# Cross-attention block on one Trainium2 core: pairs of maxima and sums in one tile, combined by VectorE instructions with one operand, in a new order of the steps

## The chip, the core and the metric

The kernel runs on one core of one Trainium2 chip. The core has five engines that each take their instructions in the order of the program: TensorE (PE; its weight loads are shown as PEld), VectorE (DVE), ScalarE (ACT), GpSimd (POOL) and SyncE (SP), which issues nearly all DMA transfers. They wait for one another through semaphores. The metric is the device time of one execution in microseconds (us), as a median over runs.

## The reference

Inputs: `x` (16 samples x 1024 rows x 512), a context of 64 rows for each sample, a condition vector for each sample, and weights. Everything is fp32.

```python
xq  = ada_ln(x,   cond, Wss_q,  bss_q)     # (1 + scale) * layernorm(x) + bias,
xkv = ada_ln(ctx, cond, Wss_kv, bss_kv)    # [scale, bias] = silu(cond) @ Wss + bss
q = (xq @ Wq + bq)                          # 16 heads of 32
k, v = split(xkv @ Wkv + bkv)
attn = softmax(q @ k.T / sqrt(32))          # over the 64 context rows
out  = x + ((attn @ v) @ Wp + bp)
```

## The kernel before

**Tiling.** `x` is cut into 32 blocks of 512 rows (`NB = 32`; block i is half of sample i // 2). The context is handled in two groups, A and B, of eight samples. A block's features are turned so that features lie on the partitions: normalised by `hidden` (L351), transposed in squares of 32 by `turn` (VectorE, L373), moved to their partitions by 16 small transfers in `move` (L392), and scaled and shifted by `scale_features` (ScalarE, L453).

**Products.** Each 512 x 512 product (query, key, value and the projection at the end) is computed as seven half-size products instead of eight, so there is a `query_product(i, n)` and a `product(i, n)` with n = 1 to 7. The price is sums and differences of quarters: `feature_sums` and `row_sums` on GpSimd, sums of weights once. Results gather in two PSUM banks for each kind: query products 1, 6, 5, 3 add into one bank, 2 and then 7, 4 into the other, and between them `query_out` (ScalarE, L583) reads a partial result or `query_added` (VectorE, L592) adds one. A product that adds into a bank waits for the reader before it. `query_seed` copies product 1 into the second bank. In the projection, `biased` and `product_seed` set the banks, `take` (ScalarE) copies partial results out, `joined` (GpSimd) or `added` (VectorE) adds them to the residual rows, and with n = 3 or 4 the finished rows are sent out.

**Softmax.** The scores of a block come in two halves w (`score_products(i, w)`, L662), each with two tiles e of two PSUM banks. The 64 context rows of a head lie on 64 partitions, two groups of 32. `maximum(i, z, e)` (L685) transposes 32x32 squares and takes the maximum over each group of 32, so there are two maxima for each query, one for each group. `copied` (L694) copies the scores out of PSUM. `exchanged(i, w)` (L722) lets ScalarE copy each group's maxima to the partitions of the other group, in four copies. `maxima(i, w)` (L732) combines the two by one VectorE instruction (L735) and spreads the result to all rows (L715). Then `subtract` (GpSimd, L739) and `weights` (exponential on ScalarE, L743). `row_total` (L749) sums over each group of 32, `sums_moved` (L762) brings the two groups' sums side by side through a round trip to DRAM, and `inverse` (L776) adds them by one instruction (L779) and takes the reciprocal (L780). `spread_rows` spreads it, `mix` (L810) multiplies weights and values on TensorE, and `divided` scales the result into `ot`, the input of the projection.

**The order.** No scheduler runs: the list of calls at the end of the function is the order of the program, and so of each engine. It has a way in (from L980: context A, keys and values, blocks 0 to 2 in part), a loop over i = 3 to 29 (L1440) and a way out (L1550, blocks y = 30 and z = 31). In a loop pass, block i has its softmax, block n = i + 1 its query product, block a = i - 1 its `mix` and most of its projection, b = i - 2 its last two projection products (3 and 4), f = i + 2 its scaling and feature differences, and blocks i + 3 to i + 5 their loading, statistics and turning. `product` 3 and 4 of block b are the second and the fourth product of a pass.

Tile buffers are few: two each for rows of `x` and for residual rows, one for the turned block `ht`, two for `xt`. The two tiles of a half's scores and the two results of `mix` share the same four PSUM banks, so `mix` waits until both score tiles were copied and their maxima taken.

## Time and profile before

| what | value |
|---|---|
| median of 3 runs | 1033.63 us (1032.38 to 1034.6) |
| the profiled execution | 1034.3 us; its span in the trace 1032.5 us |
| busy: TensorE, VectorE, GpSimd, ScalarE | 994.3, 941.0, 811.0, 779.1 us |
| mean granted TensorE clock | 0.995 |
| transfers | 151.7 MB, mean 147 GB/s |

How to read it: the profile is one execution. A row of the timeline gives the start (us from the span's start), the length, the engine, the line of the kernel, the operation, output<-inputs by tile name, and in square brackets how long the engine had been idle and what ended that. A row of the groups gives the shapes, the number of instructions, the busy time in us with the mean of one in ns, and the idle time just before them. A row of the stretches gives for each stretch the length, then the busy time of PE, PEld, DVE, ACT and POOL, the granted clock, the share of the DMA engines and GB/s. A matmul's end is modelled, and each of the program's matmuls in fp32 shows as two instructions: a half-size product is 8.

### The profile page before, as it was taken

What the parts mean: (1) busy time and instruction counts of PE and PEld (TensorE: products, weight loads), DVE (VectorE), ACT (ScalarE), POOL (GpSimd) and SP (SyncE); (2) the same over time, 40 slices, a digit from 0 to 9 for tenths busy, and PEclk for the clock granted to TensorE, in tenths of its full rate; (3) what the DMA queues carried; (4) which work ended last, traced back from release to release, by engine and by line L of the source; (5) the groups of instructions that cost most, each with busy time, mean ns of one, the idle gap of its engine ahead of it and who ended that gap; (6) DMA issues with size and microseconds to landing.
All of it is one profiled execution on the core that took longest, in us unless ns stands there. A gap on an engine that the chain in (4) does not pass through costs nothing.

```text
span 1032.5 us, 17757 instructions
## 1 busy us (share of the span) xinstructions
PE 994.3 (96%) x6060; PEld 759.1 (74%) x6060; DVE 941.0 (91%) x1170; ACT 779.1 (75%) x1426; POOL 811.0 (79%) x603
## 2 busy tenths in 40 slices
PE   6997999999999999999999999999999999999988
PEld 5875867777777777777777777777777778777657
DVE  4687999899999999999999999999999999987995
ACT  3687746788888888888878788888878788876641
POOL 1565676888888889888888889888888888887773
PEclk9999999999999999999999999999999999999989
DMA  9484633644555444544555544445554454334123
GB/s 315 146 211 114 175 102 119 186 140 139 165 168 143 134 146 154 162 130 148 166 169 129 147 148 149 157 121 164 166 165 134 127 160 157 122 113 126 44 90 125
DMA packets 111802, 151.70 MB, mean 147 GB/s; under 512 B 29624, under 2 KB 45008, under 8 KB 111712
## 3 DMA queue, kind: packets, MB, share of 16 engines
q1 hardware_dynamic: 111024, 149.75, 47.8%
q8 instruction: 48, 0.79, 0.3%
q0 software_dynamic: 256, 0.52, 0.2%
q14 instruction: 42, 0.34, 0.1%
q10 hardware_dynamic: 432, 0.30, 0.1%
HBM read 80.26 MB, written 35.65 MB: 112 GB/s over the span
## 4 chain that ended last, share of the span: by engine, by line
PE 57%; DVE 20%; issue 9%; ACT 8%; DMA 5%; SPq 1%; POOL 0%; DVEq 0%; ACTq 0%
PE pp L918 27%; PE pq L551 22%; DVE m L686 12%; ACT qt L590 4%; PE ps L669 3%; ACT mo L728 2%; DVE m L735 2%; DVE iv L780 1%; DMA x<-in_x_dram 1%; PE pv_B L551 1%; DVE lt L752 1%; PE pk_A L551 1%; DVE iv L779 1%; PE po L820 1%; DMA V_A<-stage_A 1%
## 5 line engine op out<-in xcount | busy, mean ns | idle before, releaser
L739 POOL TENSOR_TENSOR s<-s,mb 128x2048 f32<-128x2048 f32 x64 | 290.7, 4542 | 65.0 <-DVE iv L779 41.7
L695 ACT COPY s<-ps 128x1024 f32<-128x1024 f32 x128 | 129.2, 1011 | 97.2 <-DVE m L686 69.6
L918 PE MATMUL pp<-w_p_sb,ot 128*128 128x256 f32 x760 | 181.1, 382 | 6.6 <-DVE ot L806 6.6
L918 PEld LDWEIGHTS pp<-w_p_sb,ot 128*128 128x128 f32 x760 | 145.0, 191 | 29.1 <-DVE ot L806 5.4
L686 DVE TRANSPOSE_TENSOR_REDUCE m<-ps 128x32 f32<-128x1024 f32 x128 | 152.3, 1221 | 6.0 <-PE ps L669 3.1
L964 POOL TENSOR_TENSOR r<-r,taken 128x512 f32<-128x512 f32 x116 | 147.0, 1278 | 13.7 <-ACT taken L959 11.5
L715 DVE STREAM_TRANSPOSE mb<-m 128x2048 f32<-128x2048 f32 x64 | 147.9, 2312 | 7.0 <-DVE m L735 0.5
L752 DVE TRANSPOSE_TENSOR_REDUCE lt<-s 128x64 f32<-128x2048 f32 x64 | 143.5, 2273 | 1.1 <-ACT s L743 1.1
L551 PE MATMUL pq<-xt,w_q_sums 128*128 128x256 f32 x512 | 124.5, 386 | 8.1 <-ACT qt L590 8.0
L551 PEld LDWEIGHTS pq<-xt,w_q_sums 128*128 128x128 f32 x512 | 95.3, 191 | 46.3 <-ACT qt L590 32.7
L743 ACT ACTIVATE s<-s 128x2048 f32<-128x2048 f32 x64 | 122.0, 1909 | 6.0 <-POOL s L739 5.3
L551 PE MATMUL pq<-xt,w_q_sb 128*128 128x256 f32 x512 | 124.3, 386 | 1.5 <-ACT pq L563 1.5
L918 PE MATMUL pp<-WT,ot 128*128 128x256 f32 x512 | 123.8, 385 | 0.0
L551 PEld LDWEIGHTS pq<-xt,w_q_sb 128*128 128x128 f32 x512 | 94.6, 190 | 39.2 <-ACT pq L563 24.4
L551 PE MATMUL pq<-xt_sums,w_q_sums 128*128 128x256 f32 x512 | 120.8, 379 | 1.7 <-POOL xt_sums L507 1.1
L918 PE MATMUL pp<-WT,s 128*128 128x256 f32 x512 | 121.2, 379 | 0.0
L918 PEld LDWEIGHTS pp<-WT,ot 128*128 128x128 f32 x512 | 94.6, 189 | 35.0 <-issue 21.3
L590 ACT ACTIVATE qt<-pq,bias_t 128x256 f32<-128x256 f32 x256 | 104.0, 476 | 7.0 <-PE pq L551 6.9
L551 PEld LDWEIGHTS pq<-xt_sums,w_q_sums 128*128 128x128 f32 x512 | 97.1, 190 | 15.6 <-POOL xt_sums L507 1.5
L918 PEld LDWEIGHTS pp<-WT,s 128*128 128x128 f32 x512 | 97.1, 190 | 14.3 <-DVE m L735 0.8
L456 ACT ACTIVATE xt<-xt,ss_q 128x512 f32<-128x512 f32 x124 | 97.4, 809 | 6.3 <-DMA xt<-ht 6.3
L347 ACT ACTIVATE x<-x,rstdq 128x512 f32<-128x512 f32 x128 | 100.2, 808 | 2.0 <-POOL rstdq L322 1.7
(172 smaller groups left out, 1601.9 us busy)
## 6 DMA issues: line engine op xcount, KB each, us to landing
x<-in_x_dram SPq DMA_DIRECT2D x32, 1024.0 KB, 6.3
r<-in_x_dram SPq DMA_DIRECT2D x32, 1024.0 KB, 5.1
out_dram<-r SPq DMA_DIRECT2D x62, 512.0 KB, 3.7
xt<-ht SPq DMA_DIRECT2D x488, 64.0 KB, 2.4
wss_kv<-in_L_xcond_Wss_kv_dram SPq DMA_DIRECT2D x4, 512.0 KB, 8.0
wss_q<-in_L_xcond_Wss_q_dram SPq DMA_DIRECT2D x4, 512.0 KB, 8.2
ltd<-lt SPq DMA_DIRECT2D x32, 64.0 KB, 1.5
vr<-ltd SPq DMA_DIRECT2D x126, 16.0 KB, 1.7
```

The costliest lines, as they stand in the source:

```text
L347: nc.scalar.activation(dst, src, AF.Identity, bias=rstd[:, 1, j : j + 1], scale=rstd[:, 0, j : j + 1])
L456: nc.scalar.activation(xt[:, :, c, :], xt[:, :, c, :], AF.Identity, scale=ss["q"][:, c, b : b + 1], bias=ss["q"][:, NC + c, b : b + 1],)
L551: nc.tensor.matmul(out_, lhsT=lhsT, rhs=rhs, start=new and m == 0 and c == 0, stop=c == HC - 1, skip_group_check=True,)
L590: nc.scalar.activation(dst, src, AF.Identity, bias=bq_t[:, o : o + 1])
L686: nc.vector.tensor_reduce(m_tiles[i][:, z, 2 * e : 2 * e + 2, :], s_banks[i, z][e].rearrange("p r (j a) -> p r j a", a=32), AX.X, ALU.max, ...
L695: nc.scalar.copy(s_tiles[i, z][:, 2 * e : 2 * e + 2, :], s_banks[i, z][e])
L715: nc.vector.transpose(t, src.unsqueeze(2).to_broadcast([P, HPC * NJ, 32]))
L739: eng.tensor_tensor(s_tiles[i, w], s_tiles[i, w], mb_tiles[i, w], ALU.subtract)
L743: nc.scalar.activation(p, p, AF.Exp, scale=SCALE)
L752: nc.vector.tensor_reduce(lt_tiles[i][:, :, w, :], s_tiles[i, w].rearrange("p r (j a) -> p r j a", a=32), AX.X, ALU.add, apply_transpose=True,
L918: nc.tensor.matmul(acc[products_of(i, n)][:, t * HO : (t + 1) * HO], lhsT=rows[:, c, t * P : (t + 1) * P], rhs=cols[:, c, :], start=new an ...
L964: nc.gpsimd.tensor_add(r, r, taken[i][:, slot, :].rearrange("p (t h) -> p t h", t=2))
```

## The change

The tile of maxima `m2` gets one more dimension: place 0 holds a partition's own maxima, place 1 the ones that `exchanged` copies from the other group (before: two tiles, `m2` and `mo`). `maxima` combines the two places by `both` (L704, which was there and unused): a `tensor_reduce` over the pair, with one operand, in place of a `tensor_tensor` with two. `inverse` adds its two halves in the same way. All steps are the same otherwise, but the way in, the loop and the way out are listed in a new order; the same calls are made, each once. The transfers are issued at new places too: in the loop `load_x`, `sums_moved`, `move` and `load_residual` follow each other in this order at the end of a pass (before: `load_residual`, `sums_moved`, `load_x`, `move`); in the way in, half of V's move to its place (`value_move("A", 0)`) comes behind `move(2)` instead of ahead of it.

In the diff, the way in is cut to its start and two places further on, and the way out to the part around `inverse(y)` and `mix(y)`.

```diff
@@ -674,7 +674,7 @@
                     stop=True,
                 )
         if i not in m_tiles:
-            m_tiles[i] = small.tile([P, 2, HPC, NJ], F32, tag="m2", name=f"m2_{i}", bufs=2)
+            m_tiles[i] = small.tile([P, 2, 2, HPC, NJ], F32, tag="m2", name=f"m2_{i}", bufs=2)
         if i < NB - 1:
             pool, tag = big, f"big{i % 2 * 2 + w}"
         else:
@@ -684,7 +684,7 @@
 
     def maximum(i, z, e):
         nc.vector.tensor_reduce(
-            m_tiles[i][:, z, 2 * e : 2 * e + 2, :],
+            m_tiles[i][:, z, 0, 2 * e : 2 * e + 2, :],
             s_banks[i, z][e].rearrange("p r (j a) -> p r j a", a=32),
             AX.X,
             ALU.max,
@@ -717,22 +717,15 @@
 
     mb_tiles = {}
 
-    mo_tiles, mb_tiles = {}, {}
-
-    def exchanged(i, w, e=None):
-        if i not in mo_tiles:
-            mo_tiles[i] = small.tile([P, 2, HPC, NJ], F32, tag="mo", name=f"mo_{i}", bufs=2)
-        rs = slice(0, HPC) if e is None else slice(2 * e, 2 * e + 2)
+    def exchanged(i, w):
+        t = m_tiles[i][:, w]
         for k in range(4):
             o = k ^ 1
-            nc.scalar.copy(
-                mo_tiles[i][32 * o : 32 * o + 32, w, rs], m_tiles[i][32 * k : 32 * k + 32, w, rs]
-            )
+            nc.scalar.copy(t[32 * o : 32 * o + 32, 1], t[32 * k : 32 * k + 32, 0])
 
     def maxima(i, w):
         m = small.tile([P, HPC * NJ], F32, tag="m", name=f"m_{i}_{w}", bufs=2)
-        a, b = (t[i][:, w].rearrange("p r j -> p (r j)") for t in (m_tiles, mo_tiles))
-        nc.vector.tensor_tensor(m, a, b, ALU.max)
+        both(m, m_tiles[i][:, w], ALU.max)
         mb_tiles[i, w] = spread(i, m, f"mb_{i}_{w}")
 
     def subtract(i, w, eng=nc.gpsimd):
@@ -776,7 +769,7 @@
     def inverse(i):
         v = halves.pop(i)
         t = small.tile([P, 2, 2 * NJ], F32, tag="iv", name=f"iv_{i}", bufs=2)
-        nc.vector.tensor_tensor(t, v[:, :, 0], v[:, :, 1], ALU.add)
+        nc.vector.tensor_reduce(t, v.rearrange("p d z j -> p d j z"), AX.X, ALU.add)
         nc.vector.reciprocal(t, t)
         vt_rows[i] = t.rearrange("p d (w j) -> p d w j", w=2)
@@ -977,465 +970,465 @@
+    condition_turned()
+    load_first(2, 2)
     q_stats("A", (0,))
+    q_stats("A", (1,))
+    warm_up(12)
+    warm_up(6)
+    first_scale(0)
+    load_scale_shift("kv", w_ss_kv, 0, (0,))
+    load_context_weights(0, 0, 0)
+    q_stats("A", (2,))
+    hidden("A", (1,))
+    q_stats("A", (3,))
+    silu()
+    first_scale(1)
+    hidden("A", (0,))
+    turned_features("A", 0)
+    hidden("A", (2,))
+    load_scale_shift("kv", w_ss_kv, 0, (1,))
+    scale_shift_rows("kv", 0)
+    hidden("A", (3,))
+    scale_shift_taken("kv", 0)
+    load_context_weights(0, 0, 1)
+    turned_features("A", 3)
+    load_context_weights(1, 0, 0)
+    load_scale_shift("kv", w_ss_kv, 1, (0,))
     load_biases(0)
-    load_scale_shift("kv", w_ss_kv, 0, (0,))
-    condition_turned()
-    silu()
-    q_stats("A", (1,))
-    first_scale(0)
-    load_first(2, 2)
-    hidden("A", (1,))
-    hidden("A", (0,))
-    q_stats("A", (3,))
-    load_scale_shift("kv", w_ss_kv, 0, (1,))
-    q_stats("A", (2,))
-    turned_features("A", 0)
-    load_context_weights(1, 0, 0)
-    first_scale(1)
+    biases(0)
+    load_scale_shift("kv", w_ss_kv, 1, (1,))
     turned_features("A", 1)
-    scale_shift_rows("kv", 0)
-    load_scale_shift("kv", w_ss_kv, 1, (0,))
-    scale_shift_taken("kv", 0)
-    hidden("A", (2,))
-    load_context_weights(0, 0, 0)
-    warm_up(12)
-    load_scale_shift("kv", w_ss_kv, 1, (1,))
-    warm_up(6)
-    biases(0)
     scale_shift("kv", 2 * NC, 0)
-    modulated("A", 0, 0, nc.scalar)
-    turned_features("A", 2)
-    hidden("A", (3,))
     scale_shift_rows("kv", 1)
+    load_x(0)
     modulated("A", 0, 0, nc.vector)
     scale_shift_taken("kv", 1)
+    scale_shift("kv", 2 * NC, 1)
+    modulated("A", 0, 0, nc.scalar)
+    modulated("A", 1, 0, nc.vector)
+    turned_features("A", 2)
+    load_context_weights(1, 0, 1)
+    modulated("A", 0, 1, nc.scalar)
...
+    turn(2, (0,))
+    context_out("B", "k", 1)
+    hidden(2, (2,))
+    value_move("A", 1)
+    load_projection_bias()
+    score_products(0, 0)
+    scale_features(1, (0,))
+    scale_features(1, (1,))
+    scale_features(1, (3,))
+    scale_features(1, (2,))
+    turn(2, (2,))
+    feature_sums(1, nc.gpsimd, (0,))
+    feature_sums(1, nc.gpsimd, (1,))
+    maximum(0, 0, 0)
+    load_x(4)
+    context_product("B", "k", 2)
+    copied(0, 0, 0)
+    maximum(0, 0, 1)
+    context_product("B", "k", 6)
+    q_stats(3, (0,))
+    q_stats(3, (2,))
+    move(2)
+    q_stats(3, (1,))
+    query_product(1, 1)
+    copied(0, 0, 1)
+    exchanged(0, 0)
...
+    turn(3, (2,))
+    turn(3, (0,))
+    context_product("B", "k", 3)
+    query_out(1, 7)
+    query_added(1, 5)
+    scale_features(2, (3,))
     hidden(3, (3,))
-    query_product(1, 7)
-    move(2)
-    copied(0, 1, 1)
-    q_stats(4, (0,))
-    q_stats(4, (3,))
-    query_out(1, 6)
-    hidden(3, (0,))
-    maxima(0, 1)
-    scale_features(2, (3,))
-    q_stats(4, (1,))
-    query_product(1, 5)
-    query_out(1, 7)
-    turn(3, (2,))
+    context_product("B", "k", 4)
+    scale_features(2, (1,))
...
@@ -1443,254 +1436,254 @@
 
         score_products(i, 0)
         product(b, 3)
+        maximum(i, 0, 0)
+        query_product(n, 1)
         copied(i, 0, 1)
-        query_product(n, 1)
-        maximum(i, 0, 0)
+        added(b, 3)
         maximum(i, 0, 1)
+        if next_x:
+            q_stats(i + 4, (1,))
+        product(b, 4)
         copied(i, 0, 0)
         exchanged(i, 0)
-        added(b, 3)
+        score_products(i, 1)
+        query_seed(n)
         maxima(i, 0)
-        product(b, 4)
-        biased(a, 2)
-        if more:
-            hidden(i + 3, (3,))
-        score_products(i, 1)
+        maximum(i, 1, 0)
         inverse(a)
-        maximum(i, 1, 0)
         if more:
             hidden(i + 3, (1,))
         maximum(i, 1, 1)
-        query_seed(n)
-        copied(i, 1, 0)
+        subtract(i, 0)
         query_product(n, 2)
         query_product(n, 6)
-        copied(i, 1, 1)
-        subtract(i, 0)
+        query_out(n, 2)
+        query_product(n, 7)
+        copied(i, 1, 0)
+        if more:
+            hidden(i + 3, (3,))
         spread_rows(a)
         added(b, 4)
+        copied(i, 1, 1)
         mix(a)
         divided(a, (0,))
         row_sums(a, 0, (0,))
         divided(a, (1,))
+        exchanged(i, 1)
+        query_out(n, 7)
+        query_out(n, 6)
+        maxima(i, 1)
+        biased(a, 2)
+        weights(i, 0)
         row_sums(a, 1, (0,))
-        query_out(n, 2)
-        query_out(n, 6)
-        query_product(n, 5)
-        product(a, 1)
-        exchanged(i, 1)
-        weights(i, 0)
-        product_seed(a)
-        maxima(i, 1)
         if more:
             hidden(i + 3, (0,))
-        scale_features(f, (1,))
-        scale_features(f, (2,))
-        query_product(n, 7)
+        query_product(n, 4)
+        product(a, 1)
+        product_seed(a)
+        query_product(n, 5)
+        if more:
+            hidden(i + 3, (2,))
+        scale_features(f, (0,))
         if next_x:
             q_stats(i + 4, (0,))
         if more:
-            hidden(i + 3, (2,))
-        row_sums(a, 0, (1,))
-        subtract(i, 1)
+            turn(i + 3, (2,))
+        product(a, 2)
+        scale_features(f, (2,))
+        take(a, 2, 0)
+        if i == NB - 3:
+            load_residual(NB - 1)
         if more:
             turn(i + 3, (0,))
+        product(a, 6)
+        row_sums(a, 0, (1,))
+        query_added(n, 5)
+        biased(a, 3)
+        take(a, 6, 2)
+        query_product(n, 3)
+        if more:
+            turn(i + 3, (3,))
+        product(a, 5)
+        subtract(i, 1)
+        scale_features(f, (1,))
+        joined(a, 2, 0)
+        joined(a, 6, 2)
+        row_sums(a, 1, (1,))
         if next_x:
-            q_stats(i + 4, (1,))
+            q_stats(i + 4, (2,))
         if more:
             turn(i + 3, (1,))
-        if next_x:
-            q_stats(i + 4, (2,))
-        product(a, 6)
-        take(a, 6, 2)
-        query_out(n, 7)
-        product(a, 2)
-        take(a, 2, 0)
-        joined(a, 2, 0)
-        query_added(n, 5)
-        biased(a, 3)
-        joined(a, 6, 2)
-        load_residual(i)
-        product(a, 5)
+        product(a, 7)
         weights(i, 1)
         take(a, 5, 3)
-        scale_features(f, (3,))
-        if more:
-            turn(i + 3, (2,))
-        row_total(i, 0)
-        product(a, 7)
-        row_total(i, 1)
-        query_product(n, 3)
-        joined(a, 5, 3)
-        take(a, 7, 1)
-        sums_moved(i)
-        joined(a, 7, 1)
-        scale_features(f, (0,))
-        query_out(n, 3)
-        feature_sums(f, nc.gpsimd, (0,))
-        row_sums(a, 1, (1,))
         if next_x:
             q_stats(i + 4, (3,))
-        query_product(n, 4)
-        if more:
-            turn(i + 3, (3,))
+        query_out(n, 3)
         if i < NB - 5:
             load_x(i + 5)
-        if i == NB - 3:
-            load_residual(NB - 1)
+        joined(a, 5, 3)
+        scale_features(f, (3,))
+        row_total(i, 0)
+        take(a, 7, 1)
+        joined(a, 7, 1)
+        if next_x:
+            q_scale(i + 4)
+        row_total(i, 1)
+        feature_sums(f, nc.gpsimd, (0,))
         feature_sums(f, nc.gpsimd, (1,))
         query_added(n, 4)
-        if next_x:
-            q_scale(i + 4)
+        feature_sums(f, nc.gpsimd, (2,))
+        feature_sums(f, nc.gpsimd, (3,))
+        sums_moved(i)
         if i + 3 < NB:
             move(i + 3)
-        feature_sums(f, nc.gpsimd, (2,))
-        feature_sums(f, nc.gpsimd, (3,))
+        load_residual(i)
 
...
+    row_sums(y - 1, 0, (1,))
+    copied(z, 0, 0)
+    take(y - 1, 1, 0)
+    exchanged(z, 0)
+    product(y - 1, 2)
     subtract(y, 0)
-    copied(z, 0, 0)
-    product(y - 2, 4)
+    weights(y, 0)
+    take(y - 1, 2, 1)
+    row_total(y, 1)
+    maxima(z, 0)
     score_products(z, 1)
-    row_sums(y - 1, 0, (1,))
     row_sums(y - 1, 1, (0,))
-    exchanged(z, 0)
-    row_total(y, 1)
-    weights(y, 0)
-    maxima(z, 0)
-    product(y - 1, 2)
+    joined(y - 1, 1, 0)
     row_total(y, 0)
-    subtract(z, 0)
-    take(y - 1, 1, 0)
-    take(y - 1, 2, 1)
     product(y - 1, 6)
-    product(y - 2, 3)
-    biased(y - 1, 3)
     sums_moved(y)
-    take(y - 1, 6, 3)
     maximum(z, 1, 1)
     maximum(z, 1, 0)
+    product(y - 2, 4)
+    added(y - 2, 4)
+    take(y - 1, 6, 3)
+    subtract(z, 0)
+    load_residual(y)
+    biased(y - 1, 3)
     copied(z, 1, 1)
     exchanged(z, 1)
-    added(y - 2, 4)
-    added(y - 2, 3)
+    product(y - 1, 7)
+    row_sums(y - 1, 1, (1,))
+    maxima(z, 1)
+    joined(y - 1, 2, 1)
+    copied(z, 1, 0)
+    weights(z, 0)
+    inverse(y)
+    spread_rows(y, (0,))
+    take(y - 1, 7, 2)
+    spread_rows(y, (1,))
+    mix(y)
     biased(y, 2)
-    product(y - 1, 7)
-    maxima(z, 1)
     product(y - 1, 5)
-    inverse(y)
-    copied(z, 1, 0)
-    joined(y - 1, 1, 0)
-    spread_rows(y, (0,))
-    joined(y - 1, 2, 1)
-    row_sums(y - 1, 1, (1,))
-    mix(y)
+    product(y - 1, 4)
+    divided(y, (0,))
     take(y - 1, 5, 1)
-    spread_rows(y, (1,))
+    divided(y, (1,))
     subtract(z, 1)
     product(y - 1, 3)
-    divided(y, (0,))
+    product(y, 1)
     row_sums(y, 0, (0,))
-    divided(y, (1,))
-    weights(z, 0)
-    take(y - 1, 7, 2)
+    weights(z, 1)
+    row_total(z, 0)
+    product(y, 2)
+    row_sums(y, 1, (0,))
+    row_total(z, 1)
+    row_sums(y, 0, (1,))
     joined(y - 1, 7, 2)
-    row_sums(y, 1, (0,))
-    weights(z, 1)
-    product(y - 1, 4)
-    load_residual(y)
-    row_total(z, 0)
-    product(y, 1)
-    row_total(z, 1)
     added(y, 1)
+    row_sums(y, 1, (1,))
+    added(y, 2)
+    biased(y, 3)
+    joined(y - 1, 5, 1)
+    joined(y - 1, 6, 3)
```

715 lines of the change are left out of this document (341 added, 374 removed).

## The prediction

> **What bounds the kernel now.** I read the stages first: each engine's busy time in five stretches cut at starts of score products. The first ends where the first context product starts, the second is the rest of the way in, the third is loop pass i=3, the fourth passes 4 to 29, the last the way out.
>
> ```profile
> core 0: us, PE busy (x) PEld busy (x) DVE busy (x) ACT busy (x) POOL busy (x), PEclk, DMA share, GB/s
> 0.00:19.28 19.28, 9.56 (x101) 7.88 (x102) 9.03 (x33) 5.18 (x12) 1.14 (x7) 1.00 0.92 303
> 19.28:166.88 147.60, 139.35 (x808) 110.94 (x807) 124.88 (x206) 103.34 (x217) 95.95 (x90) 0.99 0.56 159
> 166.88:195.61 28.73, 28.73 (x177) 21.98 (x176) 25.71 (x32) 22.81 (x38) 20.41 (x15) 1.00 0.52 150
> 195.61:954.91 759.30, 749.54 (x4578) 569.84 (x4577) 719.79 (x842) 616.96 (x1109) 644.91 (x465) 1.00 0.48 147
> 954.91:1032.50 77.59, 67.13 (x401) 48.49 (x400) 61.61 (x59) 30.84 (x51) 48.60 (x29) 0.96 0.25 86
> ```
>
> TensorE is the bound everywhere. Pass 3 has no gap and takes 28.73 us; the 26 passes behind it take 759.30/26 = 29.20, with 759.30 - 749.54 = 9.76 us of gaps, 0.375 each. VectorE is next (719.79/26 = 27.7 a pass), then GpSimd (24.8) and ScalarE (23.7). So an order of the loop can gain about 10 us at most; the way in has 8.25 us of gaps behind its first product, the way out 10.46. Then who TensorE waited for between 200 and 920 us:
>
> ```profile
> PE pq L551 <- ACT qt L590: 7.6, 24, 0.4
> PE pq L551 <- ACT pq L563: 1.5, 1, 1.5
> ```
>
> The first row is one place in every pass. The timeline of a pass shows it, and then the same place in pass 3, where nothing waits:
>
> ```profile
> 463.21 1.27 POOL L507 TENSOR_TENSOR xt_sums<-xt 128x512 f32<-128x512 f32 x1
> 463.73 0.83 DVE L735 TENSOR_TENSOR m<-m,mo 128x64 f32<-128x64 f32 x1 [0.49 <-ACT mo L728]
> 466.53 1.99 PE L551 MATMUL pq<-xt,w_q_sb 128*128 128x256 f32 x8
> 468.81 2.14 ACT L695 COPY s<-ps 128x1024 f32<-128x1024 f32 x2 [2.48 <-DVE m L686]
> 470.18 1.95 PE L820 MATMUL po<-s,V_A 64*32 64x512 f32 x32
> 470.84 1.57 ACT L590 ACTIVATE qt<-pq,bias_t 128x256 f32<-128x256 f32 x4
> 472.47 1.99 PE L551 MATMUL pq<-xt,w_q_sums 128*128 128x256 f32 x8 [0.34 <-ACT qt L590]
> ...
> 178.00 1.95 PE L820 MATMUL po<-s,V_A 64*32 64x512 f32 x32
> 179.88 1.99 PE L551 MATMUL pq<-xt,w_q_sums 128*128 128x256 f32 x8
> ```
>
> Query product 5 behind `mix` adds into the bank that `query_out(n, 6)` reads. That read stands behind the two score copies, these behind the maxima, these behind the combination on L735, which took 0.83 us and ended at 464.56, just behind GpSimd's instruction (464.48). From `mix` to the product it is 2.29 us, without a wait 1.88.
>
> **The operation.** All executions of the two instructions that change (minimum, median, maximum in ns), then the nearest rows to what replaces them:
>
> ```profile
> L735 DVE TENSOR_TENSOR m<-m,mo x64: 193/398/1280, 82.8 to 987.7; 128x64 f32<-128x64 f32 x64
> L779 DVE TENSOR_TENSOR iv<-vr x32: 180/182/4576, 117.8 to 1012.2; 128x64 f32<-128x64 f32 x32
> L752 DVE TRANSPOSE_TENSOR_REDUCE lt<-s x64: 2267/2270/2311, 95.0 to 1002.7; 128x64 f32<-128x2048 f32 x64
> L735 DVE TENSOR_TENSOR m<-m,mo 128x64 f32<-128x64 f32 x64 | 36.2, 565 | 13.7 <-ACT mo L728 13.7
> L279 DVE COPY early<-ps_kv 128x128 f32<-128x128 f32 x2 | 0.6, 292 | 0.9 <-PE ps_kv L266 0.9
> L780 DVE RECIPROCAL iv<-iv 128x64 f32<-128x64 f32 x32 | 17.7, 553 | 1.1
> ```
>
> The form of two operands costs 0.19 us alone and up to 4.58 beside a GpSimd instruction. A reduction of one operand (L752) never strays by over 0.05 us, though GpSimd is busy for 85% of the loop. The trace has no reduction of pairs, 128x64<-128x128. Bounds: 0.19 (L735 alone) and 0.55 (L780, the slowest with 64 results); I take 0.29 from L279, which reads as many elements. VectorE saves 64 x (0.565 - 0.29) = 17.6 us, 0.55 a pass; the sums, mostly 0.18 now, lose 0.1 us each except the one of 4.58. VectorE isn't the bound, so this counts only through the chain above and the one of the way out. `exchanged` issues the same four 32x64 copies to another place: nothing changes on ScalarE.
>
> [...]
>
> **The loop, -6 us.** The new order puts query product 7 ahead of `mix` and product 4 behind it; 4 adds into the bank that `query_out(n, 7)` reads. Between the end of product 2 and that read, ScalarE does two output halves, a score copy, a normalisation, a score copy, four exchange copies and two output halves, by these means:
>
> ```profile
> L695 ACT COPY s<-ps 128x1024 f32<-128x1024 f32 x128 | 129.2, 1011 | 97.2 <-DVE m L686 69.6 <-PE ps L669 21.4
> L743 ACT ACTIVATE s<-s 128x2048 f32<-128x2048 f32 x64 | 122.0, 1909 | 6.0 <-POOL s L739 5.3
> L590 ACT ACTIVATE qt<-pq,bias_t 128x256 f32<-128x256 f32 x256 | 104.0, 476 | 7.0 <-PE pq L551 6.9
> L347 ACT ACTIVATE x<-x,rstdq 128x512 f32<-128x512 f32 x128 | 100.2, 808 | 2.0 <-POOL rstdq L322 1.7
> L728 ACT COPY mo<-m 32x64 f32<-32x64 f32 x256 | 61.9, 242 | 14.4 <-DVE m L686 11.0
> ```
>
> That is 0.95 + 1.01 + 0.81 + 1.01 + 0.97 + 0.95 = 5.70 us; four output halves back to back take 1.57 instead of 1.90 (470.84), so 5.0 is as likely. On the clock of the pass above: product 2 ends at 468.52, ScalarE is through between 473.5 and 474.2. TensorE is there at 466.53 + three products (1.73 each, 8 instructions of 216 ns) + 1.88 = 473.6. So product 4 waits 0 to 0.6 us; I take 0.15, against 0.375 now: 26 x 0.22 = 6. At the bounds the loop gains 9.8 or loses 6.
>
> What else moves in a pass, at nothing: (a) `added(b, 3)` stands between the first two maxima. Its product ends some 0.7 us behind the first maximum, so VectorE idles that long and the statistics and combination behind it are later; VectorE has 27.7 - 0.55 + 0.7 = 27.9 us to do in 28.9, and without that cover each 0.1 us is 2.6 us in all. (b) `query_out(n, 3)`, which the next score product needs, gets two products (3.45 us) for cover instead of one. (c) On SP, `sums_moved` and the 16 transfers of `move` now come ahead of `load_residual(i)`. That load of 1 MB is thus issued about 16 us into the next pass (16 such transfers took 13.51 us in a row below) and lands 5 us later; its first reader, `joined(a, 2, 0)`, stands behind `subtract(i, 1)` on GpSimd, about 23.7 us into the pass. If it came late, GpSimd and the row differences behind it would wait. (d) The feature differences go in a row at the end: GpSimd has about 3.9 us a pass to spare.
>
> **The way out, -3 us.** Timeline, and the granted clock (second figure from the end but one) behind the gap:
>
> ```profile
> 990.73 4.53 POOL L739 TENSOR_TENSOR s<-s,mb 128x2048 f32<-128x2048 f32 x1
> 990.76 4.58 DVE L779 TENSOR_TENSOR iv<-vr 128x64 f32<-128x64 f32 x1 [0.17 <-DMA vr<-ltd]
> 999.49 3.78 PE L918 MATMUL pp<-w_p_sb,ot 128*128 128x256 f32 x8 [5.04 <-DVE ot L806]
> ...
> 999.45:1006.00 6.55, 6.51 (x41) 3.18 (x41) 6.10 (x4) 0.58 (x1) 6.48 (x6) 0.57 0.02 6
> ```
>
> The sum of the halves of block 30 stood for a whole GpSimd subtraction, and inverse, spreading, division and TensorE stood behind it. With 0.29 us the chain is 4.3 us shorter. The first product behind the gap ran at a clock of 0.57, 3.78 us where 1.99 is usual: 1.8 more. Against that the new order has `mix(30)` behind 13 products of the stretch instead of 14, and its bank is free only behind `maximum(z, 1, 0)`, the exchange copies and `copied(z, 1, 0)`, at about 35.6 us into the stretch by VectorE's own list; TensorE is through at 32.1. That new wait of 3.5 us is partly the old gap moved ahead. 4.3 + 1.8 - 3.5 + 0.4 for smaller gaps is 3; bounds -7.5 (no new wait) and +3 (a wait of 5 with a slow clock behind it).
>
> How long a gap the clock stands isn't settled here: 5.04 us lowered it, 0.34 didn't. [...]
>
> **The way in, -4 us.**
>
> ```profile
> 13.42 3.05 PE L976 MATMUL warm<-ident 128*128 128x128 f32 x18
> 72.97 13.51 SPq L398 DMA_DIRECT2D xt<-ht  x16
> 88.11 0.81 ACT L456 ACTIVATE xt<-xt,ss_q 128x512 f32<-128x512 f32 x1 [4.06 <-DMA xt<-ht]
> 89.79 3.22 PE L551 MATMUL pq<-xt_sums,w_q_sb 128*128 128x256 f32 x8 [4.39 <-ACT qt L590]
> ```
>
> The 18 warm-up transposes stood between the landed weights and the bias transposes; at the front they fill idle time, so the first context product comes up to 1.8 us earlier. ScalarE stood at 88.11 for `move(2)`, with `query_out(1, 7)` behind it, and TensorE for 4.39 us and 1.3 at a low clock. In the new order half of V's move is behind `move(2)` on SP, and `query_out(1, 7)` ahead of the first scaling of block 2: 5 us go. New: context product 6 waits for the key output and so for the second bias transpose, about 2 us; nearly 60 other steps change place, which I charge 1. Together -1.8 - 5 + 3, about -4; bounds -8.25 (no gaps) and +4.
>
> **Rivals.** (1) *The loop keeps its wait*, query product 4 now waiting as 5 did: for it speaks that the same ScalarE work stands ahead of it, against it the three products of cover. The sum is then the others alone, 1034.3 - 7 = 1027. (2) *All gaps go*: 9.8 + 7.5 + 8 makes 1009. Against it: no pass but the third had none. (3) *The new form waits for GpSimd too*, so the change doesn't do what it says: L752's narrow spread speaks against it. `inverse(30)` would stand beside `subtract(z, 1)` again: -13 + 4.3 and the loop's 6 back, 1031. (4) *Slower: the weights of the second half come late*. `weights(i, 1)` (1.91 us), a take and `query_out(n, 3)` now stand in one row on ScalarE ahead of the next score product. My count has the weights start at 25.0 us of the pass, behind `subtract(i, 1)` (4.53 us on GpSimd, which three row differences now precede), and the score product due at 28.7 allows 25.1. Each 0.1 us beyond costs 27 x 0.1 = 2.7 us; from 0.5 us late on the gains are gone, at 0.8 it is 1034.3 - 13 + 22 = 1043. For it: GpSimd is busy 85% and the subtraction starts later than before; against it: ScalarE has 5 us a pass to spare.
>
> **How the numbers follow.** Against the profiled execution's own 1034.3 us (span 1032.5): -6 - 3 - 4 = -13, so 1021; it lay 0.7 above the median of the runs, so a median of 1020.5. Chances: this forecast (1012 to 1025) 0.55, rival 1 (1025 to 1031.5) 0.17, rival 2 0.08, rival 3 0.04, rival 4 0.12, and 0.04 that gains and losses cancel within 0.2%, which is 2 us and about what a measurement of this kernel can tell from no change. Faster 0.84, same 0.04, slower 0.12. The range leaves out rival 4 and the far end of rival 2: 1009 to 1032.
>
> **What would show it.** The combination at 0.2 to 0.35 us with no spread; no row of 4 us at `inverse`; TensorE's waits for L590 in the loop at under 4 us in all, passes of 28.8 to 29.0; the first scaling of block 2 without a wait of 4 us; a gap of about 3 us ahead of `mix(30)`. Wrong if passes exceed 29.2, with TensorE standing for `query_out(n, 3)` ahead of score products (rival 4), or if VectorE has no idle time left in a pass.

## The result and the profile after

The changed kernel takes 1017.95 us (median of 4 runs, 1016.57 to 1019.82), the kernel before 1034.03 us in the same comparison (4 runs, 1032.38 to 1034.6). The ratio is 0.9848, with a 95% interval of 0.9826 to 0.987. The profiled execution took 1016.95 us, with a span of 1015.1.

First the stretches of the changed kernel, cut at the same starts as those of before: first context product, first score product of block 3, first score product of block 30.

```profile
core 0: us, PE busy (x) PEld busy (x) DVE busy (x) ACT busy (x) POOL busy (x), PEclk, DMA share, GB/s
0.00:20.57 20.57, 10.59 (x106) 8.60 (x106) 10.63 (x39) 8.18 (x22) 0.70 (x6) 0.92 0.94 310
20.57:160.30 139.73, 137.13 (x805) 111.20 (x804) 120.97 (x202) 99.50 (x203) 93.81 (x88) 0.99 0.53 158
160.30:942.37 782.07, 776.91 (x4754) 593.49 (x4753) 731.48 (x872) 632.07 (x1151) 667.77 (x480) 1.00 0.51 149
942.37:1015.10 72.73, 64.19 (x401) 47.28 (x400) 57.03 (x60) 31.33 (x53) 49.59 (x30) 1.00 0.28 93
```

A stretch less TensorE's busy time in it is its gaps. So the saving splits into gaps and busy time. In the way out the busy time falls from 67.13 to 64.19 us, with the granted clock at 1.00 where it was 0.96.

| stage | before | after | difference | of it gaps | predicted |
|---|---|---|---|---|---|
| to the first context product | 19.28 | 20.57 | +1.3 | | up to -1.8 |
| rest of the way in | 147.60 | 139.73 | -7.9 | -5.65 | -2 |
| loop, 27 passes | 788.03 | 782.07 | -6.0 | -4.6 | -6 |
| way out | 77.59 | 72.73 | -4.9 | -1.9 | -3 |
| span | 1032.5 | 1015.1 | -17.4 | | -13 |

The sum of the way in was forecast at -4 and is -6.6. The total is right within 4.4 us; the experiments show that the loop's gain has another cause than the prediction gave it.

The two new instructions (groups by shape), and what TensorE waited for, in the whole span and then between 200 and 920 us:

```profile
L706 DVE TENSOR_REDUCE m<-m 128x64 f32<-128x128 f32 x64 | 17.9, 279 | 9.9 <-ACT m L724 9.9
L772 DVE TENSOR_REDUCE iv<-vr 128x64 f32<-128x128 f32 x32 | 7.9, 248 | 0.0
```

```profile
PE pq L551 <- ACT qt L590: 5.6, 27, 0.9
PE pk_A L551 <- DVE bias_t L241: 2.0, 1, 2.0
PE po L813 <- ACT s L695: 1.8, 2, 1.1
```

```profile
PE pq L551 <- ACT qt L590: 4.2, 25, 0.4
```

The combination costs 279 ns where it cost 565 on average. In the loop TensorE still waits for L590 in every pass, 4.2 us in 25 passes where it was 7.6 in 24. The timeline of a pass shows the new place: query product 4 (the last row), TensorE's first product behind `mix`, with ScalarE's exchange copies and the first two of its four output halves ahead of it.

```profile
463.24 1.95 PE L813 MATMUL po<-s,V_A 64*32 64x512 f32 x32
463.33 1.00 ACT L724 COPY m<-m 32x64 f32<-32x64 f32 x4
464.36 1.57 ACT L590 ACTIVATE qt<-pq,bias_t 128x256 f32<-128x256 f32 x4
465.34 1.97 PE L551 MATMUL pq<-xt_sums,w_q_sb 128*128 128x256 f32 x8 [0.16 <-ACT qt L590]
```

In the way in, the stall of 4.39 us is gone (ScalarE's first scaling of block 2 doesn't wait), and a wait for the bias copy has come, with a granted clock of 0.65 in the three microseconds from 28 us on (the timeline, then the stretch):

```profile
20.08 0.65 PE L411 MATMUL pxk_A<-ident,x_A 128*128 128x128 f32 x4 [1.52 <-DVE xk_A L428]
20.57 1.89 PE L551 MATMUL pk_A<-xk_A,w_k_sb 128*128 128x256 f32 x8
28.04 2.92 PE L551 MATMUL pk_A<-xk_A,w_k_sb 128*128 128x256 f32 x8 [1.96 <-DVE bias_t L241]
...
86.61 0.84 ACT L456 ACTIVATE xt<-xt,ss_q 128x512 f32<-128x512 f32 x1
```

```profile
28.00:31.00 3.00, 2.96 (x9) 2.45 (x10) 1.40 (x4) 1.90 (x7) 0.32 (x2) 0.65 1.07 371
```

In the way out `mix(30)` waits twice, and the sum of block 30's halves takes a quarter of a microsecond, just ahead of GpSimd's subtraction:

```profile
974.84 1.09 PE L813 MATMUL po<-s,V_B 64*32 64x512 f32 x16 [0.72 <-ACT s L695]
977.00 1.09 PE L813 MATMUL po<-s,V_B 64*32 64x512 f32 x16 [1.07 <-ACT s L695]
978.58 0.25 DVE L772 TENSOR_REDUCE iv<-vr 128x64 f32<-128x128 f32 x1
978.80 4.54 POOL L732 TENSOR_TENSOR s<-s,mb 128x2048 f32<-128x2048 f32 x1 [1.31 <-DVE mb L715]
```

### The profile page after: what moved, and what is told of

Read it like the earlier page. It is cut to its first block, busy times and chain, and to the rows that moved or that the text cites. A ratio compares the mean times of both kernels' runs of the same rounds, so it can differ in the third digit from the quotient of the medians.

```text
span 1015.1 us, 17766 instructions
## 1 busy us (share of the span) xinstructions
PE 988.8 (97%) x6060; PEld 760.6 (75%) x6060; DVE 920.1 (91%) x1170; ACT 771.1 (76%) x1426; POOL 811.9 (80%) x603
## 5 line engine op out<-in xcount | busy, mean ns | idle before, releaser
L911 PE MATMUL pp<-w_p_sb,ot 128*128 128x256 f32 x760 | 178.9, 379 | 0.0
L590 ACT ACTIVATE qt<-pq,bias_t 128x256 f32<-128x256 f32 x256 | 104.3, 474 | 70.6 <-PE pq L551 69.9
L686 DVE TRANSPOSE_TENSOR_REDUCE m<-ps 128x32 f32<-128x1024 f32 x128 | 155.5, 1219 | 2.1 <-ACT s L695 1.0
L695 ACT COPY s<-ps 128x1024 f32<-128x1024 f32 x128 | 126.9, 1015 | 23.6 <-POOL r L957 12.7
L551 PE MATMUL pq<-xt,w_q_sums 128*128 128x256 f32 x512 | 121.2, 379 | 0.0
L911 PEld LDWEIGHTS pp<-WT,ot 128*128 128x128 f32 x512 | 94.9, 190 | 34.6 <-issue 21.9
L551 PE MATMUL pq<-xt_sums,w_q_sums 128*128 128x256 f32 x512 | 116.5, 379 | 0.5 <-ACT qt L590 0.5
L347 ACT ACTIVATE x<-x,rstdq 128x512 f32<-128x512 f32 x128 | 103.9, 819 | 1.8 <-POOL rstdq L322 1.1
L952 ACT COPY taken<-pp 128x512 f32<-128x512 f32 x116 | 68.0, 586 | 47.3 <-PE pp L911 47.2
```

Of the source, the lines that this page charges most:

```text
L347: nc.scalar.activation(dst, src, AF.Identity, bias=rstd[:, 1, j : j + 1], scale=rstd[:, 0, j : j + 1])
L551: nc.tensor.matmul(out_, lhsT=lhsT, rhs=rhs, start=new and m == 0 and c == 0, stop=c == HC - 1, skip_group_check=True,)
L590: nc.scalar.activation(dst, src, AF.Identity, bias=bq_t[:, o : o + 1])
L686: nc.vector.tensor_reduce(m_tiles[i][:, z, 0, 2 * e : 2 * e + 2, :], s_banks[i, z][e].rearrange("p r (j a) -> p r j a", a=32), AX.X, ALU.m ...
L695: nc.scalar.copy(s_tiles[i, z][:, 2 * e : 2 * e + 2, :], s_banks[i, z][e])
L911: nc.tensor.matmul(acc[products_of(i, n)][:, t * HO : (t + 1) * HO], lhsT=rows[:, c, t * P : (t + 1) * P], rhs=cols[:, c, :], start=new an ...
```

## Experiments: the form and the order apart

The theory to be tested was that of the prediction: the one-operand form is needed, but the gain of the loop and of the way in comes from the new order, and only that of the way out from the form. The rival: the form alone does it, and the order adds little or costs. In these batches single runs of the kernel before lay between 1026.5 and 1038.4 us, so below are both the times and the stage lengths of one profile each; differences of 2 or 3 us in the times alone decide nothing.

**The form in the old order.** The kernel before, with the changed definitions:

```diff
-        nc.vector.tensor_tensor(m, a, b, ALU.max)
+        both(m, m_tiles[i][:, w], ALU.max)
...
-        nc.vector.tensor_tensor(t, v[:, :, 0], v[:, :, 1], ALU.add)
+        nc.vector.tensor_reduce(t, v.rearrange("p d z j -> p d j z"), AX.X, ALU.add)
```

> Both one-operand instructions, all steps in the order of before. Theory T (two causes, each with its own place): in the loop the combination no longer stands for GpSimd (0.565 to 0.28 us), the score copies and query_out(n, 6) come about 0.5 us earlier and most of the 0.375 us wait of query product 5 goes, 5 to 9 us; in the way out the 4.58 us at inverse(30) becomes 0.25, worth 4 to 6 us; the way in stays. 1020 to 1025 us. Rival O (the new order carries the loop): the loop stays at 29.1 us a pass and only the way out gains, 1028 to 1030 us.

Measured: 1014.76 us, ratio 0.9829 (0.9793 to 0.9864), not slower than the full change and shorter than either expectation had it. The stretches (from the first context product on) and TensorE's waits between 200 and 920 us:

```profile
18.37:164.20 145.83, 138.65 (x809) 111.05 (x808) 123.06 (x207) 103.48 (x217) 95.45 (x90) 0.99 0.58 164
164.20:942.05 777.85, 776.10 (x4754) 593.50 (x4753) 730.85 (x872) 640.08 (x1147) 664.72 (x479) 1.00 0.50 149
942.05:1012.20 70.15, 64.26 (x401) 47.36 (x400) 56.49 (x59) 30.86 (x51) 48.58 (x29) 1.00 0.27 95
```

```profile
PE pq L551 <- ACT pq L563: 1.4, 1, 1.4
PE pq L551 <- ACT qt L590: 0.2, 1, 0.2
```

The loop is 788.03 - 777.85 = 10.2 us shorter (5 to 9 were expected), with 1.75 us of gaps left, and the way out 7.4 (4 to 6). The wait for L590 that stood in every pass occurs once. The new order on top of this gave back 782.07 - 777.85 = 4.2 us in the loop and 2.6 in the way out.

**The order with the old form.** The changed kernel with the definitions of before (the diff above the other way round):

> The new order with the two-operand instructions of before. Theory T: in the new order inverse(a) stands on VectorE behind the start of subtract(i, 0) on GpSimd (4.54 us), about 1 us into it, so with two operands it waits some 3.5 us in every pass, and maxima up to 1.3 us; VectorE has about 1 us of slack a pass, so passes of 31 to 32 us and 1070 to 1110 us in all. Rival O (order carries the gain, the form of the instruction matters little): 1019 to 1024 us.

Measured: four runs of 1170.85, 1173.98, 1191.78 and 1196.3 us; the ratio is 1.1355 (1.1282 to 1.1428) by the two shorter ones. The profile is of the run of 1191.78. Groups, then the timeline of one pass:

```profile
L779 DVE TENSOR_TENSOR iv<-vr 128x64 f32<-128x64 f32 x32 | 105.0, 3280 | 0.0
L735 DVE TENSOR_TENSOR m<-m,mo 128x64 f32<-128x64 f32 x64 | 45.5, 711 | 9.9 <-ACT mo L728 9.9
```

```profile
633.15 4.53 POOL L739 TENSOR_TENSOR s<-s,mb 128x2048 f32<-128x2048 f32 x1 [1.29 <-DVE mb L715]
634.06 3.70 DVE L779 TENSOR_TENSOR iv<-vr 128x64 f32<-128x64 f32 x1
639.48 1.01 ACT L695 COPY s<-ps 128x1024 f32<-128x1024 f32 x1 [3.59 <-DVE m L686]
640.55 1.09 PE L820 MATMUL po<-s,V_A 64*32 64x512 f32 x16 [3.33 <-ACT s L695]
```

In the new order `inverse(a)` stands where `subtract(i, 0)` has just begun on GpSimd, in every pass, and with two operands it ends where that ends (637.76 and 637.68). The maxima behind it, the score copies and `mix` are late by as much. The mechanism is that of theory T, but its size was put too low (1070 to 1110 us): a pass takes 949.35/27 = 35.2 us in this profile instead of 31 to 32, with (949.35 - 844.67)/27 = 3.9 us of gaps and 2.5 us more busy time than in the full change, at a granted clock of 0.92. So this new order can only be had with the one-operand form, and the collision that the way out of before showed once is now in all passes: 32 such sums take 3280 ns on average, 182 the median before.

**The sums alone, then the maxima alone** (with the pairs in one tile), both in the kernel before and its order:

```diff
@@ inverse @@
-        nc.vector.tensor_tensor(t, v[:, :, 0], v[:, :, 1], ALU.add)
+        nc.vector.tensor_reduce(t, v.rearrange("p d z j -> p d j z"), AX.X, ALU.add)
```

> Before, with only inverse's addition in the form of one operand (32 instructions). Theory T: only the one of 4.58 us in the way out changes, with the slow clock behind it: 4 to 6 us, 1028 to 1030 us. Rival R (the gap is set by something else that is late anyway, the weights of block 31 or the residual rows): under 1.5 us, 1032.5 us or more.

```diff
@@ maxima @@
-        nc.vector.tensor_tensor(m, a, b, ALU.max)
+        both(m, m_tiles[i][:, w], ALU.max)
```

> Before, with only the maxima combined in the form of one operand (64 instructions), inverse as before. Theory T: the loop gains what e1 gains there, 5 to 9 us, way out as before: 1025 to 1029 us. Rival O: within 2 us of before.

Measured: the sums alone 1028.49 us, ratio 0.996 (0.9936 to 0.9985), as theory T has it, the loop as before (789.9) and the way out 71.44; the maxima alone 1014.61 us, ratio 0.9829 (0.9794 to 0.9864), loop 777.19, way out 70.34, so 10 us below the 1025 to 1029 expected. The timeline at the place of the 4.58 us, first with the sums changed, then with the maxima changed:

```profile
991.29 4.53 POOL L739 TENSOR_TENSOR s<-s,mb 128x2048 f32<-128x2048 f32 x1
991.52 0.29 DVE L779 TENSOR_REDUCE iv<-vr 128x64 f32<-128x128 f32 x1 [0.37 <-DMA vr<-ltd]
```

```profile
978.00 0.44 DVE L772 TENSOR_TENSOR iv<-vr 128x64 f32<-128x64 f32 x1
978.31 4.55 POOL L732 TENSOR_TENSOR s<-s,mb 128x2048 f32<-128x2048 f32 x1
```

The reduction runs in 0.29 us inside GpSimd's subtraction, where the two-operand sum took 4.58. With the maxima changed, the two-operand sum comes 0.31 us ahead of the subtraction and misses it: this is a matter of place, not of the form. The full change has the sum just as near, 0.22 us ahead, and with the old form in the new order the sum of block 30 took 0.18 us there. The maxima alone therefore bring the gain of both; of the form's two uses, the one in the loop decides.

So beside a GpSimd subtraction the two-operand sum took 4.58 us in the kernel before and 3.70 in the new order, and the reduction 0.29. Why the two forms differ there is not shown.

## Experiments: the order, stage by stage

All kernels from here on have the one-operand definitions. The steps of a stage are either those of before or those of the change.

**One stage in the new order.** The first differing steps of each stage stand for its whole list, which is in the diff of the change:

```diff
@@ way in, first kernel @@
+    condition_turned()
+    load_first(2, 2)
     q_stats("A", (0,))
...
@@ loop, second kernel @@
+        maximum(i, 0, 0)
+        query_product(n, 1)
         copied(i, 0, 1)
...
@@ way out, third kernel @@
+    copied(y, 0, 1)
+    product(y - 2, 3)
     maximum(y, 0, 0)
...
```

> The one-operand definitions with the new order of the way in alone; loop and way out in the order of before. The theory that the three orders have separate effects that add up (way in a gain of 4, loop a loss of 4 in 27 passes, way out a loss of 2.6, all against the same definitions in the order of before, 1012.2 us of span): the first score product of block 3 at 160.3 us instead of 164.2, passes of 28.81, way out 70.2, span 1008, time about 1010. The rival, that the gain of the way in is only work put off into the first passes of the loop: passes 3 to 5 are longer than 28.9 and the span is within 1 us of 1012.

> The one-operand definitions with the new order of the loop alone. If the parts add up: way in 164 us, passes of 28.94 with the wait of about 0.17 us for ScalarE's query output in each, loop 782 instead of 778, way out 70 to 71, time about 1019, so slower than the same definitions in the old order. The rival, that the new loop belongs with the new way in and was slow only at the joint with the new way out: passes of 28.81 and 1015.

> The one-operand definitions with the new order of the way out alone. If the parts add up: the two waits at mix(30) of 0.7 and 1.1 us are there, way out 72.7 instead of 70.2 us, loop 778, time about 1017. If those waits come from how the new loop hands over: no such waits, way out 70, time about 1015.

Measured: new way in 1009.5 us (ratio 0.9772, 0.9742 to 0.9803); new loop 1034.6 us (1.002, 1.0001 to 1.0039); new way out 1015.88 us (0.9835, 0.9802 to 0.9868). The stretches of the first two:

```profile
20.35:157.60 137.25, 135.45 (x806) 110.03 (x804) 120.62 (x202) 99.59 (x203) 93.47 (x88) 1.00 0.54 161
157.60:935.69 778.09, 776.42 (x4754) 593.35 (x4753) 732.68 (x872) 641.23 (x1152) 666.76 (x481) 1.00 0.50 150
935.69:1005.80 70.11, 64.26 (x401) 47.35 (x400) 56.52 (x59) 30.85 (x51) 48.59 (x29) 0.99 0.28 95
```

```profile
165.60:209.37 43.77, 31.70 (x177) 22.69 (x176) 27.67 (x34) 22.02 (x37) 19.55 (x14) 0.84 0.33 98
209.37:961.81 752.44, 748.09 (x4577) 571.63 (x4577) 702.50 (x839) 609.17 (x1110) 645.91 (x465) 1.00 0.51 148
```

The way in behaves as the first theory has it: its gain stays to the end, and the loop behind it is as short as with the old way in.

The third kernel's time lies between its expectations. The two waits at `mix(30)` are in its way out, which is 71.7 us long, 1.5 more than in the old order. To the end of TensorE's last product it takes 67.97 us, where the old order takes 66.37 and the full change 67.78: up to there the loss is that of the new order of the way out. The other 1.2 us of the change's 2.6 lie behind the last product, with only the last additions and the transfers of finished rows still to come; this tail is 3.78 us in the old order, 3.72 in the third kernel and 4.95 in the full change. The order of the loop and of the way out doesn't set it: the second kernel has 5.29, and the next one, with the same loop and way out, 3.75.

The new loop missed both expectations. Its passes 4 to 29 take 752.44/26 = 28.94 us, as in the full change, but pass 3 takes 43.77. VectorE's timeline there:

```profile
184.83 0.69 DVE L304 BATCH_NORM_STATS2 bs<-x 128x6 f32<-128x512 f32 x1 [14.31 <-DMA x<-in_x_dram]
```

**Why that pass stood.** In the new loop the statistics of block i+4 are among the first things of a pass; with the old way in the load of block 7 was issued last, at 178.31 us, behind sixteen transfers of `move(5)`. So the load was moved:

```diff
@@ way in @@
+    load_x(7)
     load_residual(2)
     sums_moved(2)
...
     move(5)
-    load_x(7)
```

> The kernel with the new loop alone, and in the order of before of the way in load_x(7) ahead of load_residual(2), sums_moved(2) and move(5) instead of last. If the 13 us that the third block's pass lost (209.4 - 165.6 = 43.8 us instead of 28.9 or so) come from the statistics of block 7, now the third thing on VectorE in a pass, waiting for a load that SP issued behind the sixteen transfers of move(5): the wait of 14 us at the first statistics goes, the first pass takes 29 to 31 us, span 1020, time about 1020. If the pass stands for something else (block 3's residual or sums): it stays at 43 and the time at 1034.

Measured: 1025.64 us (0.9921, 0.9897 to 0.9946). The wait of 14 us is gone, as expected (1.05 us is left), and the span is 13 us shorter. Pass 3 still takes 198.14 - 164.97 = 33.2 us, over the 29 to 31 expected: the transfers of the row sums, now behind the load on SP, are late for `inverse` (read back at 174.43 us, in the kernel without the move at 165.40), and through the maxima and score copies behind it `mix` is late by 1.89 us and a product slow:

```profile
177.72 0.29 DVE L772 TENSOR_REDUCE iv<-vr 128x64 f32<-128x128 f32 x1 [2.15 <-DMA vr<-ltd]
179.73 1.01 ACT L695 COPY s<-ps 128x1024 f32<-128x1024 f32 x1 [2.40 <-DVE m L686]
180.80 1.09 PE L813 MATMUL po<-s,V_A 64*32 64x512 f32 x16 [1.89 <-ACT s L695]
182.78 3.35 PE L551 MATMUL pq<-xt_sums,w_q_sb 128*128 128x256 f32 x8 [0.89 <-ACT qt L590]
```

So the time came out above the 1020 that were expected.

**The wait that the new loop keeps.** The changed kernel with one step moved:

```diff
-        exchanged(i, 1)
         query_out(n, 7)
+        exchanged(i, 1)
```

> The changed kernel with query_out(n, 7) ahead of exchanged(i, 1) in the loop's order, so that ScalarE's four exchange copies (about 1 us) no longer stand ahead of the query output that query product 4 waits for. If that wait is what the loop pays: TensorE's wait for L590 in the loop goes from 4 us to under 0.5, a pass takes 28.80 instead of 28.94, the loop 778 and the time about 1014. If ScalarE's whole queue is late and not the exchange: the wait moves to another product or to the weights of the first half and the mix, and the time stays at 1018. If maxima(i, 1) and with it subtract(i, 1) come 1.6 us later and decide: TensorE waits for ScalarE ahead of the next score product, and the kernel is slower, 1020 to 1025.

Measured: 1011.97 us, ratio 0.9793 (0.9763 to 0.9822), where the full change has 0.9848; the loop is 782.07 - 776.18 = 5.9 us shorter. The loop's stretch has practically no gap left:

```profile
162.06:938.24 776.18, 776.08 (x4754) 593.40 (x4753) 730.89 (x872) 633.37 (x1151) 667.44 (x480) 1.00 0.51 150
```

A pass is (938.24 - 191.22)/26 = 28.73 us, which is what pass 3 of the kernel before took with no gap in it. With TensorE's work as it is, no order can make the loop shorter by more than the 0.1 us of gaps that are left. The loops in the old order, in the five kernels with the maxima in the one-operand form, take 777.19 to 778.55 us, each with one wait of 1.0 to 1.6 us for `query_seed` (L563) that is absent here. So with these two steps exchanged the new order of the loop is worth 1 to 2.4 us. That the second maxima and their subtraction now stand behind `query_out(n, 7)` cost nothing.

**Put together.** Three kernels: the one above with the way out of before; the same with the second bias transpose and its copies earlier in the way in; and this way in with loop and way out of before.

```diff
@@ way in, second and third kernel @@
+    biases(1)
     feature_sums("A", nc.vector, (0,))
...
     feature_sums("A", nc.vector, (2,))
-    biases(1)
```

> The one-operand definitions, the new way in, the new loop with query_out(n, 7) ahead of exchanged(i, 1), and the order of before in the way out. If the parts add up: first score product of block 3 at 157.6 to 162 us (its three profiles so far), loop 776 (28.75 us a pass), way out 70.2, span 1004 to 1008, time about 1008, 4 below the same kernel with the new way out (1012). The rival, that the old way out was short only behind the old loop (whose mix and product order it continues): way out 72 to 73, time 1011 to 1012.

> As the kernel above it, and in the way in biases(1), the second bias transpose and its copies, ahead of the four feature sums on VectorE instead of behind three of them. If the wait of 1.5 to 2.0 us for the bias copy at the context product (about 28 us into the run) is on the path to the end: that wait is gone, no slow product behind it, everything later comes 1.5 to 3 us earlier, time about 1006. The rival, that the feature sums are then late for the next products, or that the slack is taken up by a later wait: the time stays within 1 us of the kernel above.

> The one-operand definitions, the new way in with biases(1) ahead of the feature sums, and loop and way out in the order of before. If the joints decide (the old way out is short, 70.1 us, only behind the old loop): way in 157.5 to 159 us, loop 778, way out 70.1, span 1005 to 1007, time about 1007.5, equal to the best so far (1007.9) by another split. If the early bias transpose gains a further 1.5 us on the way in of 157.6 us that the same kernel without it had: 156 us and a time of 1006.

Measured: 1010.7 us (0.9778, 0.9755 to 0.98), 1007.9 us (0.9761, 0.9739 to 0.9784) and 1009.17 us (0.9777, 0.975 to 0.9804). The first kernel's time lies just below the rival's 1011, and its way out of 72.72 us is the rival's.

Part of that is the loop ahead: the second score product waits 1.26 us for a score copy where the kernel with the old loop waits 0.47, and TensorE's last product ends 67.39 us into the way out instead of 66.37, as it does within 0.01 us in all four kernels with the new loop and the old way out. So the old way out is 1.0 us longer behind the new loop. The rest lies behind that product, and this tail varies where the order doesn't. TensorE's last product in the first kernel (span 1010.7) and in the kernel with the load moved (span 1021.4), whose way out has the same order:

```profile
1003.48 1.89 PE L911 MATMUL pp<-WT,ot 128*128 128x256 f32 x8
```

```profile
1015.76 1.89 PE L911 MATMUL pp<-WT,ot 128*128 128x256 f32 x8
```

Behind its end there are 5.33 and 3.75 us, and 3.78 in the kernel with the old loop. What makes the difference is not shown.

The early bias transpose takes the wait away and, in the second kernel, a slow product with it. TensorE in the first, then in the second:

```profile
28.09 3.08 PE L551 MATMUL pk_A<-xk_A,w_k_sb 128*128 128x256 f32 x8 [2.03 <-DVE bias_t L241]
```

```profile
24.06 2.00 PE L551 MATMUL pv_A<-w_v_sb,xk_A 128*128 128x256 f32 x8
25.89 1.89 PE L551 MATMUL pk_A<-xk_A,w_k_sb 128*128 128x256 f32 x8
```

From the first context product to block 3 the first kernel takes 141.26 us and the second 158.84 - 20.35 = 138.49. So with the wait and the slow product 2.8 us went, as expected. The third takes 158.86 - 21.77 = 137.09, beside 137.25 for the same kernel without the early transpose, which waited 1.53 us at full clock; the further gain of 1.5 us didn't come. But this pair doesn't tell what the step is worth at full clock: in the third the clock was lowered as that stretch began (0.58 in its first 2.23 us, with a first product of 2.81 us instead of 1.89), in the other it was not. The joints are as expected in the third kernel: loop 778.55, way out 70.09. The best times, 1007.9, 1009.17 and 1009.5 us, can't be told from one another; all three lie below the full change's 1017.95 and their intervals of the ratio below its own.

## Why the prediction was right, and where it was not

**The time.** 1020.5 was forecast and 1017.95 measured; faster, within the range. The stage terms were -4, -6 and -3 and came out at -6.6, -6.0 and -4.9. That the second came out exactly is chance: it is a gain of 10.2 by the form and a loss of 4.2 by the order.

**The operation.** Right: 0.29 us was taken and 0.279 measured. It doesn't wait for GpSimd (0.29 us inside a subtraction), so the third rival falls. The maxima alone, with `tensor_reduce` in place of `tensor_tensor`, brought 1014.61 us. For most of the sums the reduction is the slower form (248 ns on average, 182 the median before); what counted here was the instruction beside a busy GpSimd.

**The loop.** The length is right (28.94 us a pass, forecast 28.8 to 29.0), and so is the wait left at query product 4 (4.2 us in 25 passes, 0.17 each; 0.15 was taken, and under 4 us in all was to show it). For ScalarE's row ahead of that wait 5.0 to 5.7 us were taken; the 0.33 us saved in the output halves make it 5.4, and in the pass shown it takes 465.34 - 459.95 = 5.4 from the end of product 2. The attribution is wrong. The prediction put the gain down to the new place of product 4 and never priced the form in the order of before. Its own rows had that price: the combination ended the chain that product 5 waited 0.34 us for, and 0.83 - 0.28 = 0.55 us earlier is more than the whole wait. The runs of the form alone and of the maxima alone show that, with the loop 10.2 and 10.8 us shorter. The new order then lost 4.2 of it again, by putting four exchange copies ahead of `query_out(n, 7)`: with these two steps exchanged the loss is gone.

**What moves in a pass at nothing.** It held in the full change for all four: between 200 and 920 us TensorE waits for nothing but the row of L590 above, GpSimd doesn't wait for a residual's load, and the fourth rival, weights that come late, didn't come about. But moving the statistics to the front of a pass has a condition that the prediction did not name: the load behind them must be issued early in the way in. With the old way in it cost 13 us.

**The way out.** The collision of 4.58 us, the gap of 5.04 and the clock of 0.57 behind it are gone, TensorE's busy time falls by 67.13 - 64.19 = 2.9 us at a clock of 1.00. The mechanism is right for the old order, where the sums alone end the collision by their form. In the new order the sum stands ahead of the subtraction, so its place would have done it as well; the prediction did not see that. The mis-sized term is the new wait at `mix(30)`, 3.5 us in one piece with the clock in doubt. It is 0.72 and 1.07 us with half of `mix` between them: the copies that free its banks end at 974.79 and 976.95, 32.4 and 34.6 us into the stretch, not at 35.6, and the first half needs only the first. The clock was not lowered (1.00 from 974 to 980 us); what a wait of 3.5 us in one piece does to it was not shown. The bounds do not follow from the terms: with no new wait they add up to 4.3 + 1.8 + 0.4 = 6.5 and not 7.5, and with a wait of 5 and 1.8 for a slow clock to about nothing and not to a loss of 3.

**The way in.** The stall of 4.39 us went, as forecast; which of the two moved steps ended it no run separates. Wrong is the term of up to -1.8 us for the warm-up: the first context product comes 1.3 us later. In the new order all four turned blocks stand ahead of it, and the last waits 1.52 us for VectorE's scaled blocks; six kernels with the new way in and the one-operand form have it at 20.35 to 21.77 us (21.77 with a clock of 0.50 ahead of it), seven with the old way in at 18.37 to 19.60. The wait for the bias was forecast at 2 us and is 1.96, at context product 2 and not 6; its lowered clock was not forecast. The mis-sized term is the 1 us charged for the other steps: the gaps other than the stall and the wait for the bias were 8.25 - 4.39 = 3.86 us and are 2.60 - 1.96 = 0.64. One of them, a product that waited 1.5 us for the division, is gone with the form alone too.

**Form and order in the way in and the way out.** For the way out the prediction gave the form its share (4.3 + 1.8 us) and charged the new order 3.5; with the sums alone the way out is 6.2 us shorter, with the whole form 7.4, and the new order takes back 1.4 up to TensorE's last product. For the way in it credited the order with 4. Four profiles of the one-operand form with the unmodified new way in reach block 3 at 160.30, 157.60, 162.06 and 161.81, mean 160.4, and three with the old at 164.20, 165.60 and 163.94, mean 164.6: the order of the way in is worth some 4 us, as forecast, and of the three new orders as they stand it is the only one that gains. What the form adds there isn't clear of the scatter: the kernel before has 166.88, the sums alone 165.56, the maxima alone 166.07.

## What to carry to other kernels

When a change puts a new instruction and a new order together, price the instruction in the old order first: if what it saves on the chain exceeds the wait that it ends, the order has nothing left to gain at that wait and may open another. A step moved to the front of a loop's pass has its supplier in the stage ahead of the loop; look there for the queue on which its load is issued. And once a loop's pass is TensorE's own work (28.73 us here), only the way in, the way out and that work itself are left to work on.

## What the hardware showed that I had not expected

The granted clock fell behind a gap of 1.96 us (0.65 in the next 3 us, a product of 2.92 us where 1.89 is usual), and behind one of 2.03 a product took 3.08 us, but the clock did not fall behind one of 1.53 at the same place in the kernel with only the way in changed, whose clock was 1.00 there:

```profile
27.39 1.97 PE L551 MATMUL pk_A<-xk_A,w_k_sb 128*128 128x256 f32 x8 [1.53 <-DVE bias_t L241]
```

```profile
27.40:30.00 2.60, 2.60 (x12) 2.32 (x13) 1.89 (x4) 1.86 (x7) 0.05 (x1) 1.00 1.08 365
```

Nor does the length of a gap decide it alone. In the third of the kernels put together above the clock was at 0.50 ahead of the first context product; in the kernel with only the way in changed it was at 1.00 in the same place, and TensorE's gaps from 16 us on are 0.38, 0.41 and 1.52 us in the one and 0.39, 0.41 and 1.52 in the other. Ahead of them both had stood for 2.0 us; why the clock stayed low longer in one is not shown:

```profile
17.00:21.77 4.77, 2.84 (x34) 2.02 (x26) 3.06 (x11) 4.03 (x15) 0.96 (x1) 0.50 1.10 349
```

```profile
17.00:20.35 3.35, 1.42 (x29) 0.96 (x18) 2.83 (x10) 3.35 (x13) 0.33 (x1) 1.00 1.09 348
```

Ahead of the gap of 1.96 us, in the changed kernel, TensorE had stood for 1.52 us at 18.6 us as well, and it was busy for 2.08 of the 4 us from 24 us on; whether these earlier gaps had a part in the lowered clock isn't settled by these runs.
